# Three small moves around the attention of a two-layer kernel: table scaling behind the inner sums, a later last sum over heads, and groups of eight heads in the first batch

## The chip, the cores and the metric

The kernel runs on one core of a Trainium2 chip. The metric is the device time of one execution in microseconds. Before the change it was 2622.21 us (median of three runs, 2621.31 to 2623.85). TensorE (PE) multiplies matrices and loads its weights on a second path (PEld); VectorE (DVE), ScalarE (ACT) and GpSimd (POOL) do elementwise work; SyncE (SP) issues transfers, as do POOL and ACT. [...]

## The reference, cut to what matters

Two layers act on an image of 4 batches, 1024 channels and 32 x 32 = 1024 pixels, all in float32. The first is attention with 16 heads of 64 channels:

```python
x = hidden_states.reshape(B, C, N).transpose(0, 2, 1)
qkv = (x @ w_qkv.T + b_qkv).reshape(B, N, 3, nh, hd)
q = _rmsnorm(_apply_rope(q, cos, sin).reshape(B, N, inner), q_norm_w)   # k alike
scores = jnp.einsum('bqhd,bkhd->bhqk', q, k) * scale
attn = jax.nn.softmax(scores, axis=-1)
ctx = jnp.einsum('bhqk,bkhd->bqhd', attn, v).reshape(B, N, inner)
out = _rmsnorm(ctx @ w_proj.T, norm_out_w) + residual
```

The second is a residual block of three convolutions (1x1, 3x3, 1x1) with batch norms over all batches. The change touches the first layer alone.

## The kernel before, in words

**Stages.** For each of the four batches (`b`) the program projects q, k and v, runs the attention, and projects its result (`y`). The second layer follows when all four batches are done. Activations lie with channels on the 128 partitions. A projection of 1024 by 1024 by 1024 is done by Strassen's scheme, in the later stages twice over (`project2`): seven outer products (`k` = 0 to 6), each of seven inner ones. Some operands of a product are sums of blocks that DVE makes just before: `inner_sums` (L457 to L461) makes four sums for one `k`, the first two as part 0 and the other two as part 1. PE's third product of that `k` reads the second sum (L458).

**Rope and norm.** Of q and k the rms norm is folded into the rotary tables: when the inverse rms (`sqk` for k) has been spread over the partitions, DVE multiplies the two tables `sinT` and `cosT` by it (`tables`, L722), and then `turn(f)` (L728 or L732) applies them head pair by head pair, with a POOL transfer (L734) that adds the swapped half. After the last turn of q the tables are loaded anew from HBM by POOL (L183, L184), for k. So for batches 1 to 3 the tables' scaling for k, which happens while v is projected, comes after that load.

**The order of the work.** PE and POOL, and in most of the program DVE and ACT too, keep the order in which the program writes the instructions. `product_done` is called after each product: `after(n, step)` runs a step n products later, and `waiting` holds steps that are taken whenever a budget (`pace["room"]`) allows.

**Attention.** For each half of the queries (`c` = 0, 1) and each pair of heads (`hp` = 0 to 7), eight key tiles (`t`): PE makes scores (`sc`, L791), ACT the exponentials into one of eight places of `probs_` (`p`, L798), DVE adds them up into a tile of denominators (`den`, L815, L817; seven additions per pair), and PE multiplies them by v (`cx`, L826). The eight places are used again by the next pair of heads: an exponential waits for DVE's addition of the same place one pair before. The context of a pair comes in two halves; in batch 0 ACT copies both and a POOL transfer adds one to the other (L836).

**Denominators.** The denominators still have to be added over the 128 keys on the partitions, inverted, spread over partitions, and multiplied into the context. Two ways exist:

- Sums of four (L895): after every second pair PE multiplies two `den` tiles by ones; ACT copies the result (`rec`), SP writes it out as few rows and reads them back spread over 128 partitions (L939, L943), DVE inverts (L955), SP writes them back and spreads them to tiles `inv` (L973), and DVE multiplies (L905 or L771). The bias of v is then added by ACT (L906) in batch 0, by POOL (L772) in the others, and by DVE for the last heads.
- Sums of eight (L923, `halves`): batches 1 to 3 use them for three groups of four pairs: `halve` folds the denominators first, so that each pair takes 64 partitions. For an even pair one POOL transfer adds the tile's upper half to its lower half (L914). For an odd pair one POOL transfer copies the upper half into the place left free (L916), and a second one adds the lower half to it (L917). PE's sum of a group is queued two pairs after its last pair, in the second half of the queries (`c` = 1) one pair after.

Batch 0 before uses sums of four throughout, and keeps all its `den` tiles in two tiles of their own (`own`, in `T0` and `T2`). The very last sum of a batch (`last_inverses`) is queued half a product into the y projection, except in batch 3, where it comes directly behind the attention.

**Weight sums in batch 0.** During batch 0's attention the kernel also prepares sums of weight blocks for the later projections, in 21 parts. For each part SP loads four blocks of 256 KB (`w_blk`, `w_pre`; L390, L413), DVE makes four additions (L399 to L402, or L416 to L419), and POOL writes four blocks out (L404, L421). Four tiles are held by each of two parts; the loads of a part wait until the four writes of an earlier one have landed. Parts alternate two, one, two, one between the pairs.

Of the kernel before, what the change touches and what calls it, by code (L numbers as in the profile page):

```python
# [11 lines left out]
F32 = mybir.dt.float32  # L12
AF = mybir.ActivationFunctionType
ALU = mybir.AluOpType
# [4 lines left out]
P = 128  # L19
B, C, H, W = 4, 1024, 32, 32  # L20
N = H * W
NT = C // P
HD = 64
NHP = C // (2 * HD)
CH = 512
NCH = N // CH
# [35 lines left out]
NH = NT // 2  # L62
# [23 lines left out]
def program(ctx, tc, x, wblk, w2, w3, vecs, cos, sin, out, bad):  # L86


    nc = tc.nc
# [75 lines left out]
    with tc.tile_pool(name=f"st{u}", bufs=2) as st, ExitStack() as s:  # L165

        tp = s.enter_context(tc.tile_pool(name=f"tp{u}", bufs=1))
# [86 lines left out]
        TT = 0.21  # L254
        later, waiting = [], deque()
# [5 lines left out]
        def after(n, step):  # L261
            later.append((pace["at"] + n, step))
# [190 lines left out]
        def inner_sums(right, room, k, part):  # L453
            t1, t2, t3, t4 = room(k)
            spend(2 * TT)
            if part == 0:
                nc.vector.tensor_tensor(t1, right(k, 0, 1), right(k, 0, 0), ALU.subtract)  # L457
                nc.vector.tensor_tensor(t2, right(k, 1, 1), t1, ALU.subtract)  # L458
            else:
                nc.vector.tensor_tensor(t3, right(k, 1, 1), right(k, 0, 1), ALU.subtract)  # L460
                nc.vector.tensor_tensor(t4, right(k, 1, 0), t2, ALU.subtract)  # L461


        ahead = []

        def project2(b, which, base, right, room, spare, first, dest, tokens, tag, ready):

# [29 lines left out]
            def inner(k, part):  # L497
                t_[k] = room(k)
                inner_sums(right, room, k, part)

            def bank2(kind, name):
                return bank(kind, name).rearrange("p (q e) -> p q e", q=2)
# [213 lines left out]
        def rope(b, dst, total, eps, scale, w, tag, biased=True):  # L716

            def tables():  # L720
                for t in (sinT, cosT):
                    nc.vector.tensor_tensor(t, t, total, ALU.mult)  # L722

            def turn(f):
                k, other = dst[:, f, :], big_temp(f"{tag}s_{b}_{f}")
                for i, (t, table) in enumerate(((other, sinT), (k, cosT))):
                    if w is not None:
                        nc.vector.scalar_tensor_tensor(t, k, w[i][:, f : f + 1], table, ALU.mult, ALU.mult)  # L728
                    elif biased:
                        nc.vector.tensor_tensor(t, k, table, ALU.mult)  # L730
                    else:
                        nc.vector.scalar_tensor_tensor(t, k, col("bq", f), table, ALU.add, ALU.mult)  # L732
                for i in range(2):
                    nc.gpsimd.dma_start(dst[i::2, f, :], other[1 - i :: 2, :], accum_op=ALU.add)  # L734
                if f == NT - 1 and (b, tag) != (B - 1, "k"):
                    load_tables(nc.gpsimd)
                    pace["tables"] = pace["at"] + (4.3 if b == 1 else 3.7)

            def then():
                if pace["at"] < pace["tables"]:  # L740
                    after(pace["tables"] - pace["at"], then)
                    return
                waiting.append((4 * TT, tables))
                for f in range(NT):
                    waiting.append((4 * TT, lambda f=f: turn(f)))

            inverse_rms(total, eps, scale, f"{tag}_{b}", then)

# [25 lines left out]
        def attention(b, c, q_all, k_all, v, probs_, late, ready, extra, slow, steps_in_all, load_parts, fold, then, own):  # L774
# [1 line left out]

            at = half[c]
            sums_, contexts = [], []
            fold_two = b > 0
            homes = fold  # L780
            for hp in range(NHP):
                fold = homes if homes and hp // 4 < len(homes) else None
# [3 lines left out]
                for t in range(N // P):  # L786
                    p = probs_[:, t]
                    sc = bank("sc", f"sc_{n}_{t}")
                    for keys in (low, high):
                        for j, d in enumerate((low, high)):  # L790
                            nc.tensor.matmul(  # L791
                                sc[keys, j], k_all[d, hp, t * P + keys.start : t * P + keys.stop], q_all[d, hp, at],
                                start=True, stop=bad is not None,
                            )
                    if bad is None:
                        for j in range(2):
                            nc.tensor.matmul(sc[:, j], ones[0:1, :], rows[j], start=False, stop=True)
                    nc.scalar.activation(p, sc, AF.Exp)  # L798
                    if t == (3 if b == 0 and (c, hp) != (NCH - 1, NHP - 2) else 1) and late:
                        late.pop(0)()  # L800
                    if t in (5, 6) and biases:
                        biases.pop(0)()
                    if b == 0 and t == 2 and half_done and half_done[0][0] < c * NHP + hp:
                        half_done.pop(0)[1]()
                    if t == 1:
                        if b == 0:
                            d_ = own[hp % 4 // 2][:, hp % 2 * 2 : hp % 2 * 2 + 2, :]
                        elif fold and hp % 2 == 0:
                            d_ = fold[hp // 4][hp % 4 // 2]
                        else:  # L810
                            d_ = acc.tile([P, 2, CH], F32, tag="tot", name=f"den_{n}")
                    if t == 3:
                        load_parts()
                    if t == 1:
                        nc.vector.tensor_tensor(d_, probs[0], p, ALU.add)  # L815
                    elif t > 1:
                        nc.vector.tensor_tensor(d_, d_, p, ALU.add)  # L817
                    probs.append(p)
# [24 lines left out]
                if hp % 2 == min(b, 1) or c == NCH - 1 and (hp == NHP - 1 or fold_two and hp == NHP - 2):  # L843
                    for r in ready:
                        if b > 0:
                            mean_of_v(q_all, *r)
                        elif (c, hp) == (NCH - 1, NHP - 1):
                            mean_of_v(q_all, *r, nc.vector)
                        else:
                            mean_and_bias(q_all, *r)  # L850
                    ready.clear()
                if fold:
                    halve(hp, d_, fold[hp // 4][hp % 4 // 2])
                    if hp % 4 == 3:
                        home = fold[hp // 4]
                        eights.append(
                            (c * NHP + hp + 2 - c, lambda n=n, hp=hp, home=home: sum_of_eight(b, c, n, hp, home, ready))
                        )
# [18 lines left out]
                if (c, hp) == (NCH - 1, NHP - 1):  # L877

                    def last(ds=sums_):
                        last_inverses(b, c, hp, n, sums_of_four(n, ds), ready)  # L880

                    if b + 1 < B:
                        after(0.5, last)
                    else:
                        last()
                else:
                    late.append(lambda n=n, hp=hp, ds=sums_: inverses(b, c, hp, n, sums_of_four(n, ds), ready))
                sums_ = []
# [18 lines left out]

        low, high = slice(0, P // 2), slice(P // 2, P)

        def halve(hp, d_, home):  # L910


            if hp % 2 == 0:
                nc.gpsimd.dma_start(home[low], home[high], accum_op=ALU.add)  # L914
            else:
                nc.gpsimd.dma_start(home[high], d_[high])  # L916
                nc.gpsimd.dma_start(home[high], d_[low], accum_op=ALU.add)  # L917

        def sum_of_eight(b, c, n, hp, home, ready):

# [396 lines left out]
        for i in range(NH):  # L1317
            if i < 2:
                part = slice(0, 1) if i == 0 else slice(1, NH)
# [13 lines left out]
        for b in range(B):  # L1333
# [45 lines left out]
            def load_parts():  # L1379

                while todo and len(made) < 2:
                    made.append(todo.pop(0)(pieces, nc.sync))
# [12 lines left out]
            probs_ = xp.tile([P, N // P, 2, CH], F32, tag="x", name=f"p_{b}")  # L1395
            fold = [None, None]
            own = None
            if b == 0:
                own = [tp.tile([P, NH, CH], F32, tag=t, name=f"den_{b}_{t}") for t in ("T0", "T2")]
            if b > 0:  # L1400

                homes = [tp.tile([P, NH, CH], F32, tag=t, name=f"den_{b}_{t}") for t in ("T0", "T2")]
                fold[0] = homes = [[t[:, i : i + 2, :] for i in (0, 2)] for t in homes]
                fold[1] = homes[:1]
                if b == B - 1:
                    fold[1] = [[tp.tile([P, 2, CH], F32, tag=t, name=f"den_{t}") for t in ("cos", "sin")]]
            tc_, two = [], []

            def then(b=b, q_all=q_all, tc_=tc_, two=two):
# [24 lines left out]
            if b + 1 < B:  # L1434
# [10 lines left out]
                for i in range(0, NH, 2):  # L1445

                    def queue(b=b, i=i):
                        waiting.append((7 * TT, lambda: sums(ts[b + 1], xs[b + 1], i)))
# [268 lines left out]
        homes = {}  # L1717
# [380 lines left out]
```

## Time and profile before

| | us |
|---|---|
| median of the runs | 2622.21 |
| profiled execution, whole time | 2622.3 |
| its span, first to last instruction | 2620.5 |
| outside the span | 1.8 |
| PE busy | 2596.5 (99%) |
| DVE busy | 2126.7 (81%) |
| ACT busy | 1152.1 (44%) |
| POOL busy | 480.4 (18%) |
| attention of batch 0 | 285.8 to 514.6 |
| attention of batches 1, 2, 3 | from 857.6, 1427.3, 1995.5 |

Times in the views are counted from the first instruction of the span. A group's line gives the program's line, the engine, the operation and its tiles, the number of instructions, the busy time and the mean of one in ns, and then the idle time of that engine just before them with what ended it. A line of the timeline gives the start and the length of a run of equal instructions, and in brackets the idle time before it and its releaser. PE's matmuls overlap, so a run's length is a little more than the distance to the next run's start.

### The profile page before, as it was taken

To read this page: it belongs to the slowest core of one execution; us is meant where nothing else is said; L and a number is where in the kernel's file an instruction comes from. 1 tells how busy PE (TensorE), PEld (TensorE's weight loads), DVE (VectorE), ACT (ScalarE), POOL (GpSimd) and SP (SyncE) were. 2 spreads that over 40 slices of the span, in tenths; PEclk is the share of its full clock that TensorE was granted. 3 is DMA by queue.
4 is the path that set the end of the run, shared out by engine and by line. 5 is a ranking of instruction groups with operands and counts; after the bars stand their busy time and mean duration, and the time that the engine had idled before them with its cause. 6 is when DMAs were issued, how large, how long until landed. Compare 5 with 4: busy or idle time off the path is not lost. (4 is left out here: it accounts for less than half of the span.)

```text
span 2620.5 us, 40381 instructions
## 1 busy us (share of the span) xinstructions
PE 2596.5 (99%) x15300; PEld 1608.0 (61%) x15300; DVE 2126.7 (81%) x2579; ACT 1152.1 (44%) x1666; POOL 480.4 (18%) x634
## 2 busy tenths in 40 slices
PE   9999999999999999999999999999999999999997
PEld 4448533388888333588887333788885333855843
DVE  5577899998888876887888867888879878888977
ACT  2222466533342556333342655333334555223476
POOL 2541322201011222100011221100112323011000
PEclk9999999999999999999999999999999999999999
DMA  7897788777677444466676442656774663777176
GB/s 281 290 264 200 229 264 265 208 225 231 186 190 213 84 96 78 122 190 224 176 197 179 94 84 61 179 176 209 200 197 102 143 160 103 225 234 228 43 264 240
DMA packets 255946, 480.43 MB, mean 183 GB/s; under 512 B 32128, under 2 KB 125104, under 8 KB 255744
## 3 DMA queue, kind: packets, MB, share of 16 engines
q1 hardware_dynamic: 194896, 287.80, 35.6%
q0 software_dynamic: 52784, 173.18, 26.7%
q10 hardware_dynamic: 8064, 16.78, 1.8%
q8 instruction: 124, 2.03, 0.3%
q14 instruction: 78, 0.64, 0.1%
HBM read 334.77 MB, written 102.25 MB: 167 GB/s over the span
## 5 line engine op out<-in xcount | busy, mean ns | idle before, releaser
L798 ACT ACTIVATE p<-sc 128x1024 f32<-128x1024 f32 x512 | 479.6, 1046 | 16.6 <-PE sc L791 16.3
L791 PE MATMUL sc<-q,k 64*64 64x512 f32 x4096 | 454.8, 591 | 0.3 <-ACT p L798 0.3
L826 PE MATMUL cx<-p,to 64*64 64x512 f32 x3072 | 338.2, 589 | 0.0
L791 PEld LDWEIGHTS sc<-q,k 64*64 64x64 f32 x4096 | 150.7, 132 | 292.3 <-ACT p L798 144.9
L817 DVE TENSOR_TENSOR den_T<-den_T,p 128x1024 f32<-128x1024 f32 x192 | 236.3, 1231 | 20.4 <-DVE den_T L817 1.4
L826 PEld LDWEIGHTS cx<-p,to 64*64 64x64 f32 x3072 | 117.5, 133 | 212.1 <-issue 210.5
L817 DVE TENSOR_TENSOR den<-den,p 128x1024 f32<-128x1024 f32 x180 | 222.9, 1238 | 20.6 <-ACT p L798 2.2
L487 PE MATMUL p_v<-w_v,x 128*128 128x256 f32 x928 | 210.4, 379 | 2.6 <-DVE x L458 2.6
L492 PE MATMUL p_y<-q,w_y 128*128 128x256 f32 x928 | 210.6, 380 | 1.6 <-issue 1.6
L492 PEld LDWEIGHTS p_y<-q,w_y 128*128 128x128 f32 x928 | 175.7, 190 | 31.1 <-issue 6.6
L487 PEld LDWEIGHTS p_v<-w_v,x 128*128 128x128 f32 x928 | 176.0, 190 | 28.3 <-DVE x L458 3.8
L832 ACT COPY q<-cx 128x512 f32<-128x512 f32 x64 | 37.5, 586 | 341.2 <-PE cx L826 341.2
L492 PE MATMUL p_q<-to,w_q 128*128 128x256 f32 x672 | 152.2, 379 | 0.0
L492 PE MATMUL p_k<-to,w_k 128*128 128x256 f32 x672 | 152.2, 379 | 0.0
L492 PEld LDWEIGHTS p_q<-to,w_q 128*128 128x128 f32 x672 | 127.4, 190 | 18.4 <-issue 1.2
L492 PEld LDWEIGHTS p_k<-to,w_k 128*128 128x128 f32 x672 | 127.4, 190 | 18.4 <-issue 1.2
L826 PE MATMUL cx<-p,rq 64*64 64x512 f32 x1024 | 112.7, 589 | 0.0
L772 POOL TENSOR_SCALAR q<-q,vec 128x512 f32<-128x512 f32 x42 | 80.0, 1915 | 176.0 <-DVE q L771 176.0
L1997 PE MATMUL c<-h,w3t 128*128 128x512 f32 x256 | 110.5, 593 | 1.2 <-ACT h L1857 0.7
L734 POOL DMA_DIRECT2D k<-ks x64 | 57.7, 1089 | 182.2 <-ACT p L798 71.3
L487 PE MATMUL p_v<-w_v,t 128*128 128x256 f32 x384 | 90.1, 379 | 0.0
L492 PE MATMUL p_y<-to,w_y 128*128 128x256 f32 x384 | 90.1, 379 | 0.0
(582 smaller groups left out, 4320.5 us busy)
## 6 DMA issues: line engine op xcount, KB each, us to landing
w_v<-wd2f SPq DMA_DIRECT2D x112, 256.0 KB
w_y<-wd2f SPq DMA_DIRECT2D x112, 256.0 KB
w_q<-wd2f SPq DMA_DIRECT2D x84, 256.0 KB
w_k<-wd2f SPq DMA_DIRECT2D x84, 256.0 KB
wd2f<-w_pre POOLq DMA_DIRECT2D x68, 256.0 KB, 4.0
q<-qs POOLq DMA_DIRECT2D x64, 256.0 KB, 5.5
k<-ks POOLq DMA_DIRECT2D x64, 256.0 KB, 4.7
x1df<-y POOLq DMA_DIRECT2D x32, 512.0 KB, 5.7
```

The source lines that it names most:

```text
L487: nc.tensor.matmul(o[:, q].rearrange("p (g f) -> p g f", g=2), r[:, i, q * P : (q + 1) * P], wt[:, :, i, :], skip_group_check=True, **at,)
L492: nc.tensor.matmul(o[:, q], wt[:, q, i, :], r[:, i, :], skip_group_check=True, **at)
L734: nc.gpsimd.dma_start(dst[i::2, f, :], other[1 - i :: 2, :], accum_op=ALU.add)
L772: engine.tensor_scalar(cx, cx, col("bv", hp), None, ALU.add)
L791: nc.tensor.matmul(sc[keys, j], k_all[d, hp, t * P + keys.start : t * P + keys.stop], q_all[d, hp, at], start=True, stop=bad is not None,)
L798: nc.scalar.activation(p, sc, AF.Exp)
L817: nc.vector.tensor_tensor(d_, d_, p, ALU.add)
L826: nc.tensor.matmul(o[j * HD : (j + 1) * HD, i], v[keys, t, h0 : h0 + HD], probs[t][keys, j], start=(t == 0), stop=(t == N // P - 1),)
L832: nc.scalar.copy(cx, o[:, 0])
L1997: nc.tensor.matmul(os[i], w3t[k][:, f // NH, f % NH, :], h2[b, k][:, half[c]], start=(k == 0), stop=(k == NPT - 1),)
```

## The change

1. For k in batches 1 to 3, the tables' scaling and the turns are no longer queued when the inverse rms arrives, but kept in `behind_sums` and queued right behind part 1 of the next `inner_sums` of v's projection. The instructions of each engine, written out for both kernels, differ there in one thing: on DVE the two scalings now stand behind the four inner sums instead of ahead of them.
2. In batch 3 the last sum over heads is queued half a product into the y projection, as in the other batches.
3. Batch 0 uses sums of eight for the first twelve of its sixteen pairs, in three groups, like the other batches. The `T0` and `T2` tiles become the homes of the groups; pairs 4 and 5 of the second half keep their tiles in `T2`, the last two take tiles of the pool `acc`. On PE six sums of four leave and three sums of eight come. POOL gets 18 more transfers (six L925, six L927, six L928 in the new line numbers). The third group's scaling, and its bias of v, go to DVE behind pair 6 of the second half.
4. In batch 0 the adding transfer of an odd pair is queued only at key tile 5 of the next pair. On POOL it then stands behind the four or eight weight writes that follow the odd pair.

```diff
             def inner(k, part):
                 t_[k] = room(k)
                 inner_sums(right, room, k, part)
+                while part == 1 and behind_sums and not waiting:
+                    behind_sums.pop()()
...
-                waiting.append((4 * TT, tables))
-                for f in range(NT):
-                    waiting.append((4 * TT, lambda f=f: turn(f)))
+
+                def queue():
+                    waiting.append((4 * TT, tables))
+                    for f in range(NT):
+                        waiting.append((4 * TT, lambda f=f: turn(f)))
+
+                if b > 0 and tag == "k":
+                    behind_sums.append(queue)
+                else:
+                    queue()
...
-            fold_two = b > 0
+            fold_two = True
...
-                        if b == 0:
-                            d_ = own[hp % 4 // 2][:, hp % 2 * 2 : hp % 2 * 2 + 2, :]
+                        if own and c == NCH - 1 and hp in (4, 5):
+                            d_ = own[hp % 2]
                         elif fold and hp % 2 == 0:
                             d_ = fold[hp // 4][hp % 4 // 2]
...
+                    if t == 5 and folds:
+                        folds.pop()()
...
-                        elif (c, hp) == (NCH - 1, NHP - 1):
+                        elif c == NCH - 1 and hp >= NHP - 2:
                             mean_of_v(q_all, *r, nc.vector)
...
-                    if b + 1 < B:
-                        after(0.5, last)
-                    else:
-                        last()
+                    after(0.5, last)
...
-        def halve(hp, d_, home):
+        folds = []
+
+        def halve(b, hp, d_, home):
...
                 nc.gpsimd.dma_start(home[high], d_[high])
-                nc.gpsimd.dma_start(home[high], d_[low], accum_op=ALU.add)
+                folds.append(lambda: nc.gpsimd.dma_start(home[high], d_[low], accum_op=ALU.add))
+                if b > 0:
+                    folds.pop()()
...
-            if b == 0:
-                own = [tp.tile([P, NH, CH], F32, tag=t, name=f"den_{b}_{t}") for t in ("T0", "T2")]
-            if b > 0:
-
-                homes = [tp.tile([P, NH, CH], F32, tag=t, name=f"den_{b}_{t}") for t in ("T0", "T2")]
...
+            homes = [tp.tile([P, NH, CH], F32, tag=t, name=f"den_{b}_{t}") for t in ("T0", "T2")]
+            fold[0] = homes = [[t[:, i : i + 2, :] for i in (0, 2)] for t in homes]
+            fold[1] = homes[:1]
+            own = homes[1] if b == 0 else None
```

More of the change, by code (lines that the diff above doesn't have):

```diff
@@ L464, in program @@
         ahead = []
+        behind_sums = []
         def project2(b, which, base, right, room, spare, first, dest, tokens, tag, ready):
@@ L852, in attention @@
                 if fold:
-                    halve(hp, d_, fold[hp // 4][hp % 4 // 2])
+                    halve(b, hp, d_, fold[hp // 4][hp % 4 // 2])
                     if hp % 4 == 3:
@@ L1397, in program @@
             own = None
-            if b == 0:
-                own = [tp.tile([P, NH, CH], F32, tag=t, name=f"den_{b}_{t}") for t in ("T0", "T2")]
-            if b > 0:
-                homes = [tp.tile([P, NH, CH], F32, tag=t, name=f"den_{b}_{t}") for t in ("T0", "T2")]
[L1403 to L1406, printed above, removed]
+            homes = [tp.tile([P, NH, CH], F32, tag=t, name=f"den_{b}_{t}") for t in ("T0", "T2")]
+            fold[0] = homes = [[t[:, i : i + 2, :] for i in (0, 2)] for t in homes]
+            fold[1] = homes[:1]
+            own = homes[1] if b == 0 else None
+            if b == B - 1:
+                fold[1] = [[tp.tile([P, 2, CH], F32, tag=t, name=f"den_{t}") for t in ("cos", "sin")]]
             tc_, two = [], []
```

## The prediction

> **What bounds the kernel now.** I read the page first, then PE's waits, then the timelines where the four edits stand.
>
> ```profile
> span 2620.5 us, 40381 instructions
> ...
> PE 2596.5 (99%) x15300; PEld 1608.0 (61%) x15300; DVE 2126.7 (81%) x2579; ACT 1152.1 (44%) x1666; POOL 480.4 (18%) x634
> ```
>
> PE is the bound: 24 us of the span are without a matmul. So a microsecond can be won only by taking matmuls away or by ending one of PE's waits, and lost by giving PE a new one.
>
> ```profile
> PE p_v L487 <- DVE x L458: 2.6, 3, 1.5
> ```
>
> Of all of PE's waits this is the largest: 2.6 us in three places. The timeline of DVE shows the first of them:
>
> ```profile
> 819.70 1.22 DVE L722 TENSOR_TENSOR sinT<-sinT,sqk 128x1024 f32<-128x1024 f32 x1 [4.77 <-DMA sinT<-in_sin_dram]
> 822.01 1.23 DVE L722 TENSOR_TENSOR cosT<-cosT,sqk 128x1024 f32<-128x1024 f32 x1 [1.09 <-DMA cosT<-in_cos_dram]
> 823.15 0.69 DVE L457 TENSOR_TENSOR x<-t 128x512 f32<-128x512 f32 x1
> 823.88 0.69 DVE L458 TENSOR_TENSOR x<-t,x 128x512 f32<-128x512 f32 x1
> ```
>
> DVE stands idle for 5.9 us while the reloaded tables land, with the inner sums queued behind; PE, which wants L458, waits until 824.62. Now batch 0's attention, on PE and against a later batch:
>
> ```profile
> 314.08 3.61 PE L791 MATMUL sc<-q,k 64*64 64x512 f32 x32
> 317.62 1.06 PE L895 MATMUL dn<-den_T,ones 128*32 128x512 f32 x8
> 318.62 3.66 PE L791 MATMUL sc<-q,k 64*64 64x512 f32 x32
> 322.11 1.47 PE L826 MATMUL cx<-p,rq 64*64 64x512 f32 x12
> ...
> 933.32 7.05 PE L826 MATMUL cx<-p,to 64*64 64x512 f32 x64
> 940.29 1.07 PE L923 MATMUL dn<-den_T,halves 128*32 128x512 f32 x8
> 941.29 7.10 PE L791 MATMUL sc<-q,k 64*64 64x512 f32 x64
> 948.21 7.05 PE L826 MATMUL cx<-p,to 64*64 64x512 f32 x64
> ```
>
> From start to start, scores with a sum of four take 8.03 us and without one 6.92: a sum of four costs 1.11. A context with a sum of eight behind it takes 7.97; a plain one, 6.86 (948.21 to the next start at 955.07): also 1.11. The same stage by windows (PE, PEld, DVE, ACT, POOL, clock, DMA share, GB/s):
>
> ```profile
> 428.60:443.50 14.90, 14.90 (x140) 4.94 (x136) 14.07 (x16) 9.00 (x11) 5.17 (x9) 1.00 0.93 279
> 443.50:457.25 13.75, 13.75 (x132) 4.72 (x128) 13.13 (x15) 9.62 (x12) 3.05 (x5) 1.00 0.82 242
> 457.25:472.14 14.89, 14.89 (x141) 4.94 (x136) 13.71 (x16) 9.00 (x11) 5.17 (x9) 1.00 0.94 285
> ```
>
> PE is full, but DVE has only 0.6 to 1.2 us free per pair and the DMA engines are 82 to 94% busy. The change adds transfers just here. And POOL, around the third group's last pair:
>
> ```profile
> 458.87 0.88 POOL L836 DMA_DIRECT2D q<-cx  x1 [8.80 <-ACT cx L835]
> 459.78 2.15 POOL L404 DMA_DIRECT2D wd2f<-w_pre  x4
> 462.56 2.14 POOL L404 DMA_DIRECT2D wd2f<-w_pre  x4 [0.63 <-DVE w_pre L401]
> 473.76 0.87 POOL L836 DMA_DIRECT2D q<-cx  x1 [9.06 <-ACT cx L835]
> ```
>
> **Edit 1, the tables.** PE's idle time before L458 is 0.61 + 1.51 + 0.48 = 2.6 us. A p_v matmul is listed with 379 ns, but they follow each other every 0.22 us, so 0.16 us more of each stall lies in the modelled end: 3.1 us. With the inner sums ahead, DVE can start them when the block sums end, about 815, as PE has then left their places (at 803.33, one step earlier, the same L457 waited 0.48 us for PE). Four of them take 2.6 us; PE wants the second at 823.8. Nothing is late next: the tables still end at about 823.2, and L513, queued behind both, comes 2.5 us earlier than now. **-3.1 us**, between 0 (the wait only moves) and -3.1.
>
> **Edit 2, the last sum of batch 3.** Now PE runs the sum at 2221.13 and then loses 0.75 us until 2222.94, with the first product after it. In batch 1, ordered as the change orders batch 3, the loss behind the sum is 0.41 us (until DVE's L901 has read the context's bank). DVE's reciprocal comes about 0.45 us later; the next operand that PE takes from DVE, L458 at 2234.3, is wanted at 2236.8. **-0.3 us**, between 0 and -0.75.
>
> **Edits 3 and 4, batch 0.** On PE six sums of four leave and three of eight come: -3 x 1.11 = -3.3 us. Against it stand two terms.
>
> *The third group's wait.* Its sum is queued one pair after its last pair, behind the context that ends at 472.05 now. By then PE has lost six sums of four and gained two of eight, so it is there at 472.05 - 4.4 = 467.65. The adding transfer L928 stands on POOL behind eight weight writes. They are issued until 464.7, and the last of them lands at 469.67 (issue 464.16, 5.5 us, the longest that the trace gives for these eight; the shortest took 3.9). The queue then also carries the copy L927 ahead of them and L928 behind them. What one transfer of 256 KB costs: POOL's queue is 44.3% of 186 us busy (314 to 500) with 93 of them, 0.89 us each. So L928 lands at 469.7 + 0.9 + 0.9 to 1.5 (two adding transfers of k by halves, 289.88 and 290.44, landed 1.6 us apart) = 471.5 to 472.1; I take 471.8. PE waits 4.1 us, with the bounds 0 (a first write alone landed in 2.3 us) and 4.9. Batch 1's third group shows the wait in small:
>
> ```profile
> 1035.90 0.82 POOL L917 DMA_DIRECT2D den_T<-den  x1 [3.09 <-DMA den_T<-den]
> 1038.74 1.76 PE L923 MATMUL dn<-den_T,halves 128*32 128x512 f32 x8
> ```
>
> There the sum takes 1.69 us to the next start where the first two took 1.00. After this group batch 0 has the same PE work in both kernels, so nothing wins that time back.
>
> [...]
>
> *DVE's lateness.* L928 waits for the denominators, so any shift of DVE moves it. DVE had no idle time over 0.5 us between 321.84 and 501.9. Up to the third group's last addition, four multiplications (0.64 each) and about 1 us of small reciprocals with their waits leave or move behind it: -3.2 with starts. Against that, DVE's single weight parts wait for loads that follow the writes. By the semaphores in the trace their loads land 1.21, 1.13, 0.49, 1.29 and 1.54 us before DVE takes them (361.90, 389.67, 417.44, 445.46, 473.57). Without the two multiplications ahead (1.28) the first, second and fourth have nothing left; the third and fifth gain 1.28. Copy and half an adding transfer lengthen each chain by 0.9 + 0.4 = 1.3 us: three stalls of 1.4, 1.3 and 0.9, and 0.9 at 321.84, where one fold transfer goes ahead of the awaited writes. Sum -3.2 + 4.5 = **+1.3**; the bounds are -3.1 (all of it hidden) and +6.7 (2.5 us per chain, where an adding transfer takes 1.6 and is counted in full).
>
> POOL's issues themselves (0.55 to 0.87 us each, 18 of them) lie in its idle time: 5.2 of 14.9 us busy. The third group's four biases, 0.4 us each on DVE instead of ACT, fall in the 2.3 us that DVE idles at 501 to 504; without that cover they would meet PE at the y projection, where L901 has 1.25 us to spare. SP's longer lists wait for later sums, but no load behind them is due before: free.
>
> So batch 0: -3.3 + 4.1 + 1.3 = **+2.1**, between -2.7 and +8.3.
>
> **Sum.** -3.1 - 0.3 + 2.1 = -1.3. The profiled execution took 2622.3 (span 2620.5 and 1.8 outside), 0.1 above the median: **2621.0 us**.
>
> **The rivals.**
>
> *The fold is hidden after all (faster).* L928 lands in time and the DMA engines have room. For it: the engines move up to 360 GB/s in slices of this stage, against a mean of 265. Then batch 0 gives -3.3 less 0.65 for DVE, which ends only 1.4 us earlier where PE ends 3.3 earlier and 1.25 are to spare: -2.7. Total -6.1: 2616.2.
>
> *DMA becomes the bound of batch 0 (slower).* 18 transfers x 0.89 = 16 us in 186 us bring 88% to 96% busy. If each chain grows by 3 us or more, DVE is late by 8 us at the third group, batch 0 loses 9 and the total is +5.7: 2628. It decides from about 2.8 us per chain. Against it: 2.5 us is already the sum of all that queues ahead.
>
> *The tables' wait only moves.* L513 or the turns hold PE instead: -0.3 + 2.1 = +1.8: 2624.1. Against it: DVE's order is otherwise the same, and DVE is ahead.
>
> **How the numbers follow.** A measurement tells about 0.2% (5.2 us) from no change: 2617.0 to 2627.4. Main case 0.46 (its own range 2618 to 2624); fold hidden 0.26; DMA-bound 0.17; the wait moves 0.11. Only the second lies below 2617.0 and only the third above 2627.4: faster 0.26, same 0.57, slower 0.17. The range runs from just under the fold hidden (2616.2), 2615.6, to the edge of the DMA-bound case, 2627.5.
>
> **What would show it.** The wait of p_v for L458 gone from PE's list. A wait of PE before the third group's sum (about 468 to 472), and DVE waiting for weight loads at the parts named. DMA share near 0.96 in batch 0. If the third sum starts at 468 without a wait, the first rival holds; if DVE idles over 2 us at each single part, the second.

## The result and the profile after

The changed kernel takes 2639.77 us (median of six runs, 2637.01 to 2644.11), the kernel before 2621.76 (2619.91 to 2623.85): a ratio of 1.0071, with a 95% interval of 1.006 to 1.0082. It is 18 us slower, where 1.3 us less was predicted. The profiled execution took 2638.62.

```profile
span 2636.8 us, 40340 instructions
...
PE 2598.1 (99%) x15276; PEld 1608.0 (61%) x15276; DVE 2129.7 (81%) x2580; ACT 1149.9 (44%) x1659; POOL 492.9 (19%) x652
```

PE is busy 1.6 us longer with 24 instructions fewer, and the span has grown by 16.3. PE's waits name the places (engine, line, what it waited for; us in total, times, longest):

```profile
PE dn L936 <- DVE den_T L829: 10.5, 1, 10.5
PE sc L801 <- ACT p L808: 5.3, 4, 4.3
...
PE p_y L493 <- issue: 1.2, 3, 0.4
```

The three waits of p_v for L458 are gone, and the longest wait of p_y is 0.4 us for 0.8. Two new ones stand in batch 0. Laid side by side, the starts of PE's stages show that batch 0's attention alone takes 19.2 us longer, and that the rest gains some 3.5 us at the tables. The timeline of PE around the two waits:

```profile
412.42 2.75 PE L801 MATMUL sc<-q,k 64*64 64x512 f32 x24
419.50 7.26 PE L801 MATMUL sc<-q,k 64*64 64x512 f32 x40 [4.32 <-ACT p L808]
...
475.93 1.05 PE L936 MATMUL dn<-den_T,halves 128*32 128x512 f32 x4
487.53 1.92 PE L936 MATMUL dn<-den_T,halves 128*32 128x512 f32 x4 [10.54 <-DVE den_T L829]
489.38 9.04 PE L801 MATMUL sc<-q,k 64*64 64x512 f32 x64
```

The third sum of eight stops half-way: its first four matmuls read the home of two pairs, the others wait for the home that L928 completes. POOL shows why that is late:

```profile
469.18 0.55 POOL L927 DMA_DIRECT2D den_T<-den  x1 [4.60 <-DVE den L829]
471.24 2.16 POOL L404 DMA_DIRECT2D wd2f<-w_pre  x4 [1.51 <-DVE w_pre L401]
479.28 2.13 POOL L404 DMA_DIRECT2D wd2f<-w_pre  x4 [5.88 <-DVE w_pre L401]
481.40 0.90 POOL L928 DMA_DIRECT2D den_T<-den  x1
```

L928 leaves at 481.40 (it lands at 487.44 by the semaphores), behind four weight writes that waited for DVE, and DVE in turn waited for a weight load:

```profile
414.04 0.69 DVE L399 TENSOR_TENSOR w_pre<-w_pre,w_pre 128x512 f32<-128x512 f32 x1 [5.08 <-DMA w_pre<-in_wblk_dram]
...
476.84 0.69 DVE L399 TENSOR_TENSOR w_pre<-w_pre,w_pre 128x512 f32<-128x512 f32 x1 [5.18 <-DMA w_pre<-in_wblk_dram]
```

The DMA queues and kinds from 314 to 500 us (packets, MB, share of 16 engines), first of the kernel before:

```profile
q0 software_dynamic: 8412, 24.81, 44.3%
q1 hardware_dynamic: 24075, 24.27, 42.9%
```

then of the changed kernel:

```profile
q0 software_dynamic: 9107, 27.30, 52.2%
q1 hardware_dynamic: 20337, 21.47, 38.4%
```

POOL's queue carries 2.5 MB more, SP's, with the weight loads, 2.8 MB less in the same time: the loads of the weight sums are all there (76 in both kernels), but four spreading transfers and the six loads of `w_y` that come last before are missing, as the stage has become late. Now the windows of batch 0 by stretch (start and end; length, then busy time of PE, PEld, DVE, ACT, POOL; PE's granted clock, DMA share, GB/s), before:

```profile
385.00:400.00 15.00, 15.00 (x147) 5.15 (x143) 14.27 (x16) 9.62 (x12) 3.03 (x5) 1.00 0.90 275
400.00:414.00 14.00, 14.00 (x132) 4.62 (x128) 13.17 (x16) 9.00 (x11) 5.17 (x9) 1.00 0.91 269
```

and after:

```profile
385.00:400.00 15.00, 15.00 (x148) 5.16 (x144) 12.94 (x14) 9.60 (x13) 5.13 (x8) 1.00 1.07 300
400.00:414.00 14.00, 14.00 (x136) 4.86 (x132) 8.44 (x9) 8.42 (x11) 3.59 (x6) 1.00 1.01 280
429.00:445.00 16.00, 16.00 (x152) 5.25 (x148) 15.10 (x18) 11.04 (x14) 5.81 (x10) 1.00 0.71 203
```

The DMA engines are full (1.07, 1.01, in a count that can pass 1) while DVE waits (12.94, then 8.44 us busy), and at 0.71 once DVE has its data. So the mean of 88%, read as room for 18 more transfers, was no room: where the transfers stand together there is none.

### The profile page after: what moved, and what is told of

It is laid out like the page before. It is cut to its first block, busy times and chain, and to the rows that moved or that the text cites. A ratio compares the mean times of both kernels' runs of the same rounds, so it can differ in the third digit from the quotient of the medians.

```text
span 2636.8 us, 40340 instructions
## 1 busy us (share of the span) xinstructions
PE 2598.1 (99%) x15276; PEld 1608.0 (61%) x15276; DVE 2129.7 (81%) x2580; ACT 1149.9 (44%) x1659; POOL 492.9 (19%) x652
## 4 chain that ended last, share of the span: by engine, by line
PE 86%; DVE 6%; DMA 5%; issue 1%; ACT 1%; POOL 0%; SPq 0%; DVEq 0%; ACTq 0%; POOLq 0%
PE sc L801 14%; PE cx L838 14%; PE p_y L493 13%; PE p_v L488 12%; PE p_q L493 10%; PE p_k L493 10%; PE c L2007 3%; PE c L1717 3%; PE pa_q L310 2%; DMA w_pre<-in_wblk_dram 1%; PE c L1070 1%; PE pc_q L310 1%; PE pa_k L310 1%; PE c L1028 1%; PE c1s L1070 1%
## 5 line engine op out<-in xcount | busy, mean ns | idle before, releaser
L829 DVE TENSOR_TENSOR den<-den,p 128x1024 f32<-128x1024 f32 x228 | 281.7, 1236 | 26.3 <-ACT p L808 2.2
L829 DVE TENSOR_TENSOR den_T<-den_T,p 128x1024 f32<-128x1024 f32 x144 | 177.6, 1233 | 15.3 <-DVE den_T L827 0.5
```

## The experiments

Three questions were open: what makes DVE wait (SP's order, POOL's order, or time on the DMA engines), whether PE's wait of 10.5 us or DVE's lateness is the price, and what the other edits are worth. For each run, DVE's ledger of batch 0 is given, from the first denominator's addition to the first operand of the y projection: length of that stretch, DVE's busy time in it, and the rest, its idle time. It is read from lines like these two, of the kernel before and of the changed one (columns as above):

```profile
292.01:513.09 221.08, 221.08 (x2044) 74.70 (x2040) 202.77 (x218) 140.80 (x173) 63.31 (x106) 1.00 0.84 247
291.98:532.30 240.32, 225.07 (x2020) 74.78 (x2016) 205.25 (x219) 138.30 (x166) 77.56 (x124) 0.96 0.87 247
```

| kernel | time | 95% interval of the ratio to before | length | DVE busy | DVE idle |
|---|---|---|---|---|---|
| before | 2621.76 | | 221.1 | 202.8 | 18.3 |
| changed | 2639.77 | 1.006 to 1.0082 | 240.3 | 205.3 | 35.1 |
| edits 1, 2 | 2619.42; 2619.18 | 0.9983 to 1.0001; 0.9982 to 1.0 | | | |
| edit 1 | 2619.93 | 0.9985 to 1.0003 | | | |
| edits 3, 4 | 2643.42 | 1.0067 to 1.0098 | 245.7 | 205.3 | 40.4 |
| spread later on SP | 2640.43 | 1.006 to 1.0091 | 241.7 | 205.3 | 36.5 |
| no fold transfers | 2621.06 | 0.999 to 1.0009 | 223.5 | 204.6 | 18.9 |
| quarter transfers | 2625.26 | 1.001 to 1.0029 | 227.8 | 205.0 | 22.8 |
| third sum a pair later | 2646.16 | 1.0077 to 1.0111 | 240.0 | 200.8 | 39.1 |
| without edit 4 | 2649.47 | 1.0092 to 1.0126 | 252.2 | 205.3 | 46.9 |
| no fold transfers, biases on ACT | 2618.62 | 0.9983 to 1.0001 | 220.6 | 202.8 | 17.7 |

The runs of before beside them had medians of 2621.63 (beside edits 1 and 2 the first time, edits 3 and 4, the later spreading, and no fold transfers), 2620.74 (beside the quarter transfers, the later third sum, and the kernel without edit 4) and 2621.2 (beside edit 1, edits 1 and 2 the second time, and the biases on ACT).

**Edits 1 and 2 alone, and edits 3 and 4 alone.** The first is the kernel before with the parts of the diff on `behind_sums` and `after(0.5, last)`; the second is the changed kernel with these undone.

> The kernel before with edits 1 and 2 alone; batch 0 as before. The stages of the two traces, laid side by side, give -0.9, -1.8 and -0.84 us at the three table scalings and about -0.2 at the last sum: -3.7, so near 2618. If the gain of edit 1 is taken back by work behind it, 2621 to 2622. If batch 0 owes something to edits 1 and 2, this run cannot show it, but the next one does.

> The changed kernel with edits 1 and 2 undone, so that edits 3 and 4 stand alone. If the parts add up, +19 to +20 us over before: near 2641, with PE's waits of about 4 us (scores, for ACT's exponentials) and about 10 us (third sum of eight) as in the changed kernel. If they depend on one another, under 2637 or over 2645.

Edits 1 and 2 took 2.2 us off, a little less than expected, with an interval that just holds no change; edits 3 and 4 alone added 21.8. The sum, 19.6, is near the 18.0 of all four. PE's wait before the third sum was 15.2 us in that run (10.5 with all four) and DVE's idle time 40.4 us (35.1), although edits 1 and 2 leave batch 0 alone: so such waits vary from build to build, and single differences of a few microseconds in the ledger say little. Edit 1 is undone there, and still PE waits for L458 only once, 0.7 us, where the kernel before has 2.6 us in three places: what edit 1 can remove varies too. The loss lies in edits 3 and 4.

**SP's order.** In batch 0 the spreading was to go behind the next weight loads (`spreads` holds the loop that stood there):

```diff
                 nc.sync.dma_start(rows, few)
-                for i in range(2):
-                    ...
-                    spread(c, hp - 2 + 2 * i, n + f"_{i}", ready, ...)
+                def spreads():
+                    ...
+                if b == 0:
+                    to_spread.append(spreads)
+                else:
+                    spreads()
...
                     if t == 3:
                         load_parts()
+                        while to_spread:
+                            to_spread.pop(0)()
```

> In batch 0 the four spreading transfers of a sum of eight are queued on SP behind the next weight loads and no longer ahead of them; they wait for the landing of the rows (L944, 7.2 us), and the loads stood behind that wait. Everything else, all transfers included, is as in the changed kernel. Theory A (order on SP): the loads of the two parts that DVE waited 5.1 and 5.2 us for are issued 6 us earlier, both waits fall below 2 us, PE's wait of 4.3 us for the exponentials goes and that of 10.5 us before the rest of the third sum falls to about 4 us: 2624 to 2629. Theory B (load on the DMA engines: it is the added transfers that make all landings longer): both DVE waits stay above 4 us and the time stays at 2636 to 2641.

Nothing moved: DVE's waits were 6.6 and 6.6 us, the time 2640.43. But the run says little of theory A, as the trace shows the four transfers in their old place on SP (398.00 to 399.83, the loads from 400.53). SP is not among the engines whose order the program writes out, and the edit did not change its order. In the changed kernel, the loads of the first long wait were issued at 403.97 to 405.56, directly behind the spreading, while the writes that they wait for had landed at 401.65 to 403.54. At the second long wait the loads left at 465.34 to 468.14, for writes landed at 463.35 to 465.48. So some 2 to 2.7 us of either wait are SP's order at most. The next runs decide the rest.

**No fold transfers, and a quarter of each.** First `halve` returns at once for batch 0; then it keeps all transfers, on 16 partitions instead of 64:

```diff
+        low4, high4 = slice(0, P // 8), slice(P // 2, P // 2 + P // 8)
...
+            lo, hi = (low4, high4) if b == 0 else (low, high)
             if hp % 2 == 0:
-                nc.gpsimd.dma_start(home[low], home[high], accum_op=ALU.add)
+                nc.gpsimd.dma_start(home[lo], home[hi], accum_op=ALU.add)
...
```

> The 18 transfers of the fold in batch 0 are left out (so the denominators of its first twelve pairs are wrong); PE, DVE, ACT and SP keep all their instructions. Theory A (order on SP): the DVE waits of 5 us are still there, a little shorter (3 to 5 us each), PE's third sum waits for nothing but DVE: 2625 to 2632. Theory B (load on the DMA engines): both waits go, batch 0 is left with three sums fewer on PE, and the time falls to 2614 to 2618.

> The 18 transfers of the fold in batch 0 keep their places on POOL and in its queue, but each moves 16 partitions where it moved 64 (so the denominators of the first twelve pairs are wrong): 64 KB for 256 KB. Theory B1 (time on the DMA engines): three quarters of some 16 us of transfers go, DVE's waits of 5 us fall below 1.5 us, PE waits under 2 us: 2619 to 2625. Theory B2 (the order on POOL and in its queue, where weight writes stand behind transfers of the fold, whatever their size): the waits stay above 4 us, 2634 to 2640.

Without the transfers the time is that of before again, and no wait of DVE behind the first (322 us) is over 0.9 us. With a quarter of the bytes, and POOL's order and SP's as in the changed kernel, 4.5 of the 18 us remain. Against the run without transfers the quarter costs 5.1 us and the whole 18.6 (each taken against its own runs of before: -0.6, +4.5, +18.0). So the price roughly follows the bytes: on the average 1.03 us per transfer of 256 KB, a little over the 0.89 us that one takes on the engines in the kernel before. Theory B1 holds in the main, and A falls: SP's lists are the same in the quarter run. But 2625.26 lies just outside B1's 2619 to 2625, and two of its sizes were missed. PE still waited for the third sum:

```profile
PE dn L938 <- DVE den_T L829: 6.3, 1, 6.3
```

That is after a wait of DVE of 3.5 us for a load, until 464.51, which was expected under 1.5.

Theory B had expected 2614 to 2618 without the transfers, since three sums less are left for PE. That did not come: 2621.06. The trace shows PE 5 to 6 us ahead of before at 459 us, and then two new waits:

```profile
PE p_y L493 <- DVE q L910: 1.8, 1, 1.8
PE dn L904 <- DVE den_T L829: 1.8, 1, 1.8
```

PE gets no more than DVE has ready; DVE finishes batch 0's attention 2.4 us after the time of before, counted from its own start.

**The four biases.** As the run without transfers, but the third group's biases on ACT:

```diff
-                    if t in (5, 6) and biases:
+                    if t in ((3, 4, 5, 6) if (c, hp) == (NCH - 1, NHP - 1) else (5, 6)) and biases:
...
-                        elif c == NCH - 1 and hp >= NHP - 2:
+                        elif (c, hp) == (NCH - 1, NHP - 1):
                             mean_of_v(q_all, *r, nc.vector)
```

> As the run without the fold's transfers (denominators of batch 0's first twelve pairs wrong as there), but the third group's four biases are added by ACT as before, not by DVE. There DVE ended batch 0 at 514.1, 1 us later than before, with 2.0 us of these biases in it, and PE waited 1.8 us at the y projection. If DVE is what ends batch 0 once the transfers are gone, that wait goes and the time falls by 1.5 to 2 us from 2621.1 to about 2619.3. If the biases lie in idle time, as the prediction had it, the time stays at 2621.

2618.62, so 2.4 us less (2.0 with each taken against its own runs of before), and the wait of p_y is gone. The intervals of the two runs overlap, so the time alone does not settle it, but the ledger agrees: 1.8 us less of work for DVE, a stretch 3.0 us shorter. By these signs the biases did not lie in idle time.

**PE's wait or DVE's lateness.** Two edits to the changed kernel: the third sum one pair later in batch 0, and the adding transfer queued at once.

```diff
-                            (c * NHP + hp + 2 - c, lambda ...)
+                            (c * NHP + hp + 2 - (c if b else 0), lambda ...)
...
-            half_done.append((c * NHP + hp + 3 - c, invert))
+            half_done.append((c * NHP + hp + 3 - (c if b else 0), invert))
```

```diff
                 folds.append(lambda: nc.gpsimd.dma_start(home[high], d_[low], accum_op=ALU.add))
-                if b > 0:
-                    folds.pop()()
+                folds.pop()()
```

> The changed kernel with the third group's sum of batch 0 (and what follows it) queued one pair of heads later, as the first two groups' are. PE's 10.5 us wait before that sum should go. Theory D (DVE is what is late: in batch 0's attention it idles 35.1 us where it idled 18.3 before, and PE can't run ahead of the denominators): the wait comes back in the scores that follow, which wait for exponentials and these for places of probs_; batch 0 stays 15 to 19 us longer than before and the time is 2634 to 2640. Theory P (PE's wait at the sum is a price of its own): the 10.5 us and the slow restart behind it go, 2626 to 2629.

> Edit 4 undone: the adding transfer of an odd pair goes out right behind the copy, ahead of the four or eight weight writes. Theory D (DVE's waits for weight loads set the end): the writes land later by one transfer, 0.9 to 1.6 us, at each of six odd pairs, DVE's idle time grows, and the earlier landing of L928 (by some 3 us at the third group) is given back: 2638 to 2646. Theory P (PE's wait for L928 sets the end): PE's 10.5 us wait falls to 6 or 7 us and the time to 2634 to 2637.

With the later sum, PE's 10.5 us wait is gone and nothing is won. PE's waits in that run:

```profile
PE sc L801 <- ACT p L808: 9.7, 4, 4.8
PE p_y L493 <- issue: 6.7, 4, 5.5
PE dn L904 <- DVE den_T L829: 4.4, 1, 4.4
```

The wait has moved to the scores and to a sum of four, and batch 0's attention is as long as ever (240.0 us). So theory D is right on the wait and theory P falls. But D's 2634 to 2640 missed 2646.16. The third group's scaling now lies in the y projection (from 534.25 us; from 518.25 in the changed kernel), on DVE ahead of the reciprocal of the last sum (540.98 for 537.68). The last scaling (L781) comes at 558.12 for 549.52, and p_y lost another 5.5 us behind it.

Without edit 4 the kernel is 10 us slower still, beyond even D's range. POOL's waits from 314 to 500 us show what is new:

```profile
POOL den_T L928 <- DMA den_T<-den: 28.0, 6, 7.1
```

The adding transfer writes where the copy L927 has just been written, so POOL holds it until the copy has landed, 4.7 us in the mean, with the weight writes behind. In the changed kernel, where L928 stands behind the writes, this wait is 0.0: the copy has landed by then. The half pair of delay keeps the fold from being worse.

**Edit 1 alone, and edits 1 and 2 once more.**

> The kernel before with edit 1 alone. The traces gave -0.9, -1.8 and -0.84 us at its three places: -3.5, so 2617 to 2618.5 beside a before of 2621 to 2621.6. If a part of the gain is taken back later in the same stages (DVE's next sums, or the turns), -1 to -2.

> The kernel before with edits 1 and 2 once more, on another chip perhaps, to narrow an interval that just held 1: -2.2 us measured the first time, -3.7 expected from the traces. Against edit 1 alone, edit 2 should give -0.2 to -0.4, which these runs can hardly tell from nothing.

Edit 1 alone 1.3 us less, both 2.0 less; none of the three intervals excludes no change, though all medians lie below. In the traces all three waits for L458 are gone in each of the three runs. From 351 us on, behind the first projections, in which these traces differ by up to 1 us, PE's stages gain 3.5, 3.0 and 2.5 us up to the attention of batch 3 (first run with both edits, edit 1, second run with both).

## Why the prediction was wrong

**What bounds the kernel.** "PE is the bound" holds for the whole, but in batch 0's attention DVE is a second bound, with 18.3 us idle in 221, most of it in gaps under half a microsecond. I had the 0.6 to 1.2 us free per pair on the page, and still counted PE's matmuls as won time. The three sums less, -3.3 us, brought 0.6 by the medians (the last run of the table, which also has edits 1 and 2, against these two alone beside the same runs of before: 2618.62 to 2619.18), which is within the noise.

**Edit 1: right.** -3.1 predicted, 2.5 to 3.5 in the traces, 1.3 to 2.2 in the medians, with edit 2 or without. DVE does what was foreseen. In the run of edits 1 and 2 alone, where the times can be laid beside those of before, the inner sums start at 815.00 ("about 815"; behind the waiting tables, in the kernel before, at 823.15), the tables end at 823.26 ("about 823.2"), and L516, the old L513, follows 2.5 us earlier than before:

```profile
815.00 0.69 DVE L457 TENSOR_TENSOR x<-t 128x512 f32<-128x512 f32 x1 [0.48 <-PE p_v L488]
815.73 0.69 DVE L458 TENSOR_TENSOR x<-t,x 128x512 f32<-128x512 f32 x1
...
819.17 1.22 DVE L725 TENSOR_TENSOR sinT<-sinT,sqk 128x1024 f32<-128x1024 f32 x1 [1.55 <-DMA sinT<-in_sin_dram]
822.03 1.23 DVE L725 TENSOR_TENSOR cosT<-cosT,sqk 128x1024 f32<-128x1024 f32 x1 [1.63 <-DMA cosT<-in_cos_dram]
823.17 1.28 DVE L516 TENSOR_TENSOR to<-to,p_v 128x512 f32<-128x512 f32 x2
```

**Edit 2: right in its mechanism.** The loss at the sum fell from 0.75 to 0.41 us, as in the other batches; -0.3 is too little to be seen in the time.

**DVE's lateness, +1.3 (bounds -3.1 and +6.7): the step that failed.** Measured is 19.2 us: 16.8 more of idle time and 2.5 more of work. Of the stalls foreseen, those at the single parts came about as written (1.9, 1.2 and 1.6 us for 1.4, 1.3 and 0.9; the slack listed there gives 1.4, 1.4 and 1.3, half a microsecond more in all). But two of 5.1 and 5.2 stand at second parts of doubles, which I had left out because their loads had 2.8 to 3.8 us of slack (3.5 and 3.4 at these two), and the one near 322 grew by 3.8 instead of 0.9. I had asked only what a transfer adds to the queue ahead of one load. But weight loads, DVE's additions and weight writes form a ring, in which each waits for the one before: a load lands later, so the writes come later, so the next loads are issued later. At the second long wait the last load lands at 476.72 us, DVE takes it at 476.84, the writes leave at 479.28 and land from 483.93 on, and the next loads leave from 483.98 on. On the average each of the 18 transfers made the ring later by about its own time (1.03 us for 0.89), and nothing later in the batch won it back. That the same transfers would cost less with more buffers in the ring was not tried.

**The third group's wait, 4.1 us (bounds 0 and 4.9): 10.5.** From issue to landing L928 took 6.0 us, somewhat less than I had reckoned (464.7 to 471.8). But it was issued at 481.40, 16.7 us later, as the weight writes ahead of it waited for DVE, and PE, held back by its first stall, reached the sum only 8 us later (475.93 for 467.65). As the later sum showed, this wait is a sign of DVE's lateness and no price of its own.

**What I called free.** SP's longer lists: their part is small, at most 2 to 2.7 us at a long wait, though a run that changed SP's order alone was not had. The four biases in "2.3 us that DVE idles": 1.8 of them had been DVE waiting for exponentials, and so for PE's scores, and vanished with PE's earlier arrival; the biases cost about 2 us once the transfers are gone.

**The rivals.** "DMA becomes the bound of batch 0" comes nearest to what happened: 18.6 us over six chains are 3.1 on the average, above its point of decision (about 2.8 us per chain). But it charged 9 us for them: it let only 8 us of the lateness reach DVE. And the sign given for it did not come: at the single parts DVE idled 1.2 to 1.9 us, not over 2, as the long waits stood elsewhere. Nor did the share of 0.96 foreseen for the DMA engines: from 314 to 500 us it was 0.91, for 0.88 before, as the work took longer. "The fold is hidden" was wrong twice: the transfers are not hidden, and even without them PE's three sums are not won.

From issue to landing the twelve copies and adds of an odd pair took 7.1 us in the median, and in the run with 64 KB each still 5.4. That is far more than the 0.89 us that one transfer took on the engines in the kernel before; I put the rest down to the queue at the engines, which no run shows by itself. The fold's transfers were added to POOL's queue alone, and SP's loads did not all suffer: its 28 loads of `w_pre` from the input landed in 7.3 us in the median for 4.8 before, but its 40 loads from `wdf` in 4.6 for 5.4. Why the ones came later and the others did not was not shown.

## What to carry to other kernels

A mean DMA share of 88% was no room here: look at the share in the phases in which an engine waits for a load (1.07 and 1.01 here), and count an added transfer there at its full time on the engines (here 0.89 us, and 1.03 paid), for each one, where loads, additions and writes form a ring with few buffers. Before counting matmuls as won, see whether a second engine is nearly full in the same stage (here DVE, busy 202.8 of 221.1 us); its ledger (length, busy, idle) told at once what each variant cost. A wait that is moved away and comes back elsewhere with the stage as long as before (here 10.5 us gone, and 240.0 us for 240.3) was a sign and not a cause.

The version to keep is the kernel before with edits 1 and 2: 2619.3 us, 20 less than the changed kernel, and 2 less than before by medians, at the edge of what these runs can tell.

## What was not expected of the hardware

PE ran at half its clock behind two stalls. Windows of the changed kernel behind them (4.3 and 10.5 us; columns as above):

```profile
419.50:425.30 5.80, 5.80 (x28) 1.77 (x32) 5.38 (x5) 4.16 (x5) 0.92 (x2) 0.52 1.05 263
425.30:431.00 5.70, 5.70 (x60) 1.98 (x56) 5.60 (x9) 3.85 (x5) 1.04 (x2) 1.00 0.79 224
487.50:493.50 6.00, 5.97 (x24) 1.51 (x28) 5.80 (x9) 1.92 (x3) 0.00 (x0) 0.51 0.62 190
493.50:499.50 6.00, 6.00 (x60) 2.02 (x56) 5.41 (x5) 6.00 (x8) 2.18 (x4) 1.00 0.69 225
```

For 5.8 and 6.0 us the granted clock is 0.52 and 0.51, and PE does about half the work (28 and 24 matmuls, for 60 in the windows that follow): an estimated 2.9 us lost each time. After a stall of 3.8 us, in the run without edit 4, it stayed at 1.00; after one of 5.4 there it fell to 0.52. In the trace of the changed kernel the granted clock is 0.50 from 418.24 to 425.07 us and from 479.68 to 493.33 us, and 1.00 on the other side of each of these times. PE was back at full clock 5.6 and 5.8 us after its restarts (419.50 and 487.53). So a stall of 4.3 us cost the clock here and one of 3.8 us did not; what decides it was not shown. In this kernel the slow stretches probably cost little, though no run tests it, since DVE was the late one: it was busy 5.38 of 5.80 and 5.80 of 6.00 us in them.
